# Opening turns, beta additions and the keys' pace reordered in a graph attention and top-p diffusion kernel

## Chip, cores and metric

The kernel runs on one core of one Trainium2 chip. The metric is device microseconds of one execution, and the time of a kernel is the median of its runs. A profile comes from one execution, and its span, the time between the program's first and last instruction, is somewhat shorter than that execution's own time.

## What is computed

There are 4096 nodes with 256 features each, and two layers. Both layers normalize the rows of x, apply a ReLU, and add their result to x. The first is a graph attention with four heads over the matrix adj; the second mixes plain graph diffusion (`Xf = R @ Xf`) and top-p attention over all nodes (`Xa = A @ Xa`), two steps of each.

```python
# layer 0, on h = relu(layernorm(x))
h = (h @ W).reshape(n, 4, 64)
src = einsum('nhd,d->nh', h, a[:64, 0]); dst = einsum('nhd,d->nh', h, a[64:, 0])
e = src[:, :, None] + dst.T[None, :, :]
e = where(adj > 0, where(e > 0, e, 0.2 * e), -9e15)
out = einsum('nhm,mhd->nhd', softmax(e, axis=-1), h)      # then
x = x + layernorm(out) * gamma + beta
# layer 1, on X = relu(layernorm(x)), Xf = Xa = X, Z = 0
R = row_normalized(adj + I)
for n in range(2):
    A = top_p_attention(Xa, W1, W2, W3)      # softmax(q k^T), the largest probabilities up to 0.9, renormalized
    Xf = R @ Xf
    Xa = A @ Xa
    Z = Z + Xf @ U1[n].T + Xa @ U2[n].T
x = x + layernorm(X + Z) * ln_g + ln_b
```

## The kernel before

The rows are held as 32 blocks of 128 (`NB`), in one tile `X` of 128 partitions. The order of every engine's instructions is the order in which the Python code issues them, since nearly all of it stands inside `tc.manual_schedule`; the framework adds the semaphore waits. What the code issues ahead of something else on the same engine is therefore executed ahead of it. SP's queue carries most loads and stores, POOL's queue the adjacency loads.

**The opening.** One turn (`turn_of(b)`) per block, and each turn works on several blocks at different stages: `opened(b + 2)` normalizes and rectifies a block on ACT (L233), `turned_rows(b + 1)` transposes it on PE (L240), `multiplied(b)` copies the transposed rows on ACT (L244) and multiplies them by `wx` on PE (L247). `wx` holds W and, in eight further columns, W times the two halves of `a`, which DVE works out first (L512, L514). `read(b - 1)` takes the eight logits out of PSUM (DVE, L251, into `sd_c`) and makes two exponentials per head of them (ACT, L254); `weighed(b - 1)` multiplies the block's rows by these (DVE, L259). `first_part`, `left`, `second_part` and `third_part` split the weighted rows in three bf16 parts (L263 and L270 on ACT, L267 on DVE, L275 on DVE and POOL), which POOL copies into `ut0` for head 0 (L276) and SP's queue stores for the other heads (L277). `measured(b + 8)` takes a block's moments (DVE, L149 and L150), and after each fourth block POOL makes the scales (`steps`, L141 to L144). Between turns 13 and 27, eight pieces of the first two sign tiles are made on POOL (`sign_stage` with a piece, L359).

**The attention passes.** For each group of 8 row blocks (`ig`) and each head there is one pass, 16 in all, each with 16 steps over pairs of neighbour blocks. A sign tile tells where `src + dst > 0` (ACT, L366, or DVE, L364); DVE ands it with the adjacency tile `ax` and takes the rest (L372, L373, two masks); PE multiplies both masks by the weighted rows into 8 PSUM banks (L392). Masks are made two steps ahead and signs three. `evacuate` empties the banks after a pass, and its later pieces wait in the list `later`, of which one is issued per step. After the last head of a group they include `closing(ig)`: moments of the rows (`stats`), then for each of 8 blocks `close(i)`, which normalizes (ACT, L441), multiplies by gamma (DVE, L442), adds beta to the old rows (POOL, L443), adds both (DVE, L444), stores `x1` (SP's queue) and takes moments, and then `relu` (ACT, L452). The last group's closing runs beside the first graph hop.

**The graph hops.** A hop has 4 passes over column groups of 8 blocks, with 32 steps each. `split` makes two parts of a block of rows, `hl` (L579 on ACT, L580 on DVE); `edge` loads a strip `ar` of the adjacency from DRAM (SP's queue, L572); `own` adds the identity (L589); PE multiplies (L602). At a pass's end `drained` copies four banks (L613) and, in the next pass, its rows are turned (L624).

**Beside the hop** the top-p attention is prepared by two generators, `fills` and `picks`; each half step of the hop advances `fills` by one `yield` and, except near the pass's end, `picks` too. `fills` begins with `projections`: for each of 8 groups of 4 blocks it transposes (L752 and L753), multiplies by the key and query weights (L759, L761), transposes keys and queries (L766, L768, L769) and takes their lengths. `yield from waits(k)` between these pieces sets their pace; n is the number of the diffusion step. Then follow the moments (L784), the tables, and logits and exponentials of the first three blocks, for which `picks` searches the threshold on DVE. After the hop, `attend` does the rest block by block.

Of the kernel before, what the change touches and what calls it, by code (L numbers as in the profile page):

```python
# [11 lines left out]
F32 = mybir.dt.float32  # L12
F32R = mybir.dt.float32r
# [13 lines left out]
P = 128  # L27
# [29 lines left out]
def gat_then_top_p_diffusion(  # L57
# [104 lines left out]
    with tc.tile_pool(name="l0", bufs=1) as l0, tc.tile_pool(name="l0s", bufs=2) as l0s, tc.tile_pool(name="l0o", bufs=1) as l0o:  # L162
# [26 lines left out]
        with tc.manual_schedule(engines=every | {ET.SP}):  # L189
# [31 lines left out]
            def measured(b):  # L221
                if b < NB:
                    if b % 4 == 0:
                        pro.mv = l0s.tile([P, 4, nc.vector.BN_AGGR_DIM], F32, name="mv4")
                    moments_of(pro.mv[:, b % 4, :], X[:, b, :])
                    if b % 4 == 3:
                        pro.scales[b // 4] = steps(pro.mv, 4, l0s)

            def opened(b):
                if b < NB:  # L230
                    rs, nmr = pro.scales[b // 4]
                    hb = pro.hb[b] = l0s.tile([P, D], F32, name="hb", tag="ob")
                    nc.scalar.activation(hb, X[:, b, :], AF.Relu, scale=rs[:, b % 4:b % 4 + 1], bias=nmr[:, b % 4:b % 4 + 1])  # L233
# [15 lines left out]
            def read(b):  # L249
                pm, uv = pro.pm[b], uvs[b % len(uvs)]  # L250
                nc.vector.tensor_scalar(sd_c[:, :, :, b], pm[:, ds(D, 2 * H)].rearrange("p (t h) -> p t h", t=2),  # L251
                                        TINY, -TINY, ALU.add, ALU.add)
                for t, scale in enumerate((1.0, ALPHA)):
                    nc.scalar.activation(uv[:, :, t, HD:], pm[:, ds(D + H, H)][:, :, None], AF.Exp, scale=scale)  # L254

# [47 lines left out]
            def turn_of(b):  # L303
# [34 lines left out]
        out_rows = {}  # L338
        later = []

        def sources(k):
# [11 lines left out]
        def signs(k, p, g=None, piece=None):  # L353

            g = g or l0m.tile([P, 2, G0 * P], U8, name="g", bufs=5)
            h = passes[k][1]
            if piece is not None:
                c, half = piece // 2, ts(piece % 2, G0 * P // 2)
                nc.gpsimd.tensor_scalar(g[:, c, half], shared[k].sr[:, half], d_neg[:, h, ds(2 * p + c, 1)], 255.0, ALU.is_gt, ALU.mult)  # L359
# [36 lines left out]
        def evacuate(k):  # L396
# [27 lines left out]
            return [three, divided] + (closing(ig) if h == H - 1 else [])  # L424

        def closing(ig):
            o = out_rows[ig]
# [9 lines left out]
            def close(i):  # L437
# [4 lines left out]
                nc.vector.tensor_mul(ob, ob, gamma_r)  # L442
                nc.gpsimd.tensor_tensor(xb, xb, beta_r, ALU.add)  # L443
                nc.vector.tensor_add(xb, xb, ob)  # L444
# [61 lines left out]
        with tc.manual_schedule(engines=every):  # L506
            for b in range(4):
                measured(b)
            for k in range(KC):
                for i in range(2):  # L510
                    pr = uvs[3 + i][:, :, 0, :HD]
                    nc.vector.tensor_mul(pr, wx[:, k, :D].rearrange("p (h d) -> p h d", h=H),  # L512
                                         a_r[:, None, ts(i, HD)].to_broadcast([P, H, HD]))
                    nc.vector.reduce_sum(wx[:, k, ds(D + i * H, H)], pr, axis=AX.X)  # L514
            for b in range(4, 8):
                measured(b)
# [10 lines left out]
            for n, (k, p) in enumerate(todo):  # L527
# [18 lines left out]
        ps1 = ctx.enter_context(tc.tile_pool(name="ps1b", bufs=2, space=PSUM))  # L546
        PASSES = NB // G0
        S = SimpleNamespace(spare=None)

        order = [(p, j) for p in range(PASSES) for j in range(NB)]  # L550

        def hop_of(hop):
            return SimpleNamespace(hop=hop, src={}, ar={}, hl={}, acc=None, begun=0, parted=0, owned=0)

        def source(A, n):
            if n in A.src or n >= len(order):
                return
            if A.hop == 0:
                A.src[n] = X[:, order[n][1], :]
            else:  # L560
                A.src[n] = S.rows.tile([P, D], F32, name="x1", bufs=3) if n % 5 < 3 else S.rows.tile([P, D], F32, name="xa")
                nc.sync.dma_start(A.src[n], xf_d[order[n][1]])

        def edge(A, n):
# [8 lines left out]
            A.ar[n] = ar  # L573

        def split(A, n):
            while A.parted < min(n, len(order)):
                src = A.src[A.parted]
                hl = rp.tile([P, 2, D], F32R, name="hl", bufs=5)
                nc.scalar.copy(hl[:, 0, :], src)  # L579
                nc.vector.tensor_tensor(hl[:, 1, :], src, hl[:, 0, :].bitcast(F32), ALU.subtract)  # L580
                A.hl[A.parted] = hl
                A.parted += 1

# [80 lines left out]

        first_hop = hops(hop_of(0))
        with tc.manual_schedule(engines=every | {ET.SP}):
# [50 lines left out]
    def waits(n):  # L717
        for i in range(n):
            yield

    def projections(cur, n, G):
# [25 lines left out]
        for g in range(NB // 4):  # L747
            xs = l1e.tile([P, 3, 4, P], F32, name="xs", tag="e1")
            for k in range(KC):
# [3 lines left out]
                nc.scalar.copy(xs[:, k], pt)  # L753
            yield from waits(1 + n)
            carried(xs, g, 0)
# [7 lines left out]
            carried(xs, g, 1)  # L763
            yield from waits(n)
            for i in range(4):
# [9 lines left out]
            carried(xs, g, 2)  # L775
            yield from waits(n)
            carried(xs, g, 3)
# [668 lines left out]
```

## Time and profile before

| What | us |
|---|---|
| Median of 3 runs (2898.01 to 2899.80) | 2899.59 |
| The profiled execution's own time | 2899.5 |
| Its span | 2897.7 |
| PE busy in it | 2814.0 (97%) |
| DVE busy | 2171.2 (75%) |
| ACT busy | 1914.8 (66%) |
| POOL busy | 878.6 (30%) |

The trace shows the stages in the order of time: the opening up to about 102 us, the attention passes to 810, the first hop with what stands beside it to 1124, the first top-p attention to about 1806, the second hop to about 2200, the second attention to the end. A busy share is an average over stages with different limits. In the profile's rows, a number in brackets with an arrow is how long the engine stood idle before an instruction, and what ended that; PEld is PE's weight load.

### The profile page before, as it was taken

The page shows a single profiled execution, that of the slowest core. Times are in us where ns is not written, and L with a number is a line of the kernel's source. Part 1 is how long each engine was busy: PE and PEld are TensorE (multiplying, and loading weights), DVE is VectorE, ACT ScalarE, POOL GpSimd, SP SyncE. Part 2 cuts the span into 40 slices and gives each one's busy share as a digit, 9 for nine tenths or more (in the row PEclk, how much of TensorE's full clock was granted, in tenths as well). Part 3 has the DMA queues.
Part 4 walks back from the last instruction along what each step waited for, and adds up shares of the span by engine and source line. Part 5 has one row for each costly group of instructions (what it writes and reads, how often), then busy time and mean ns, then how long its engine had stood idle before and what let it go on. Part 6 is the DMA issues. An engine that isn't in the chain of part 4 may idle for free. (4 is left out here: it accounts for less than half of the span.)

```text
span 2897.7 us, 51524 instructions
## 1 busy us (share of the span) xinstructions
PE 2814.0 (97%) x18777; PEld 2443.1 (84%) x18777; DVE 2171.2 (75%) x5069; ACT 1914.8 (66%) x3061; POOL 878.6 (30%) x1815
## 2 busy tenths in 40 slices
PE   6899999999999999999999999999999999999998
PEld 4799999999977778888888888767778888888887
DVE  7776877778654374888888889234474999999996
ACT  6786787868733634877788775222626777877782
POOL 6501211112010120233323331000204666666664
PEclk8899999999999999999999999999999999999999
DMA  7969577595454784000000000667992111111110
GB/s 177 217 247 223 187 227 195 211 224 187 177 189 158 238 298 164 20 20 26 20 20 20 26 20 19 231 197 236 313 352 68 31 31 38 34 31 31 39 31 25
DMA packets 190362, 376.48 MB, mean 130 GB/s; under 512 B 18192, under 2 KB 143120, under 8 KB 186000
## 3 DMA queue, kind: packets, MB, share of 16 engines
q1 hardware_dynamic: 146960, 275.12, 28.4%
q0 software_dynamic: 21504, 83.89, 12.2%
q10 hardware_dynamic: 21632, 14.05, 1.5%
q8 instruction: 152, 2.49, 0.3%
q14 instruction: 114, 0.93, 0.1%
HBM read 305.55 MB, written 113.57 MB: 145 GB/s over the span
## 5 line engine op out<-in xcount | busy, mean ns | idle before, releaser
L1075 PE MATMUL acc<-X,eT 128*128 128x256 f32 x4096 | 973.7, 383 | 3.3 <-ACT eT L1069 2.8
L1075 PEld LDWEIGHTS acc<-X,eT 128*128 128x128 f32 x4096 | 739.0, 190 | 111.4 <-ACT eT L1069 31.4
L392 PE MATMUL acc<-ut,m 128*128 128x195 bf16 (+1 forms) x8192 | 701.0, 247 | 8.2 <-DVE st L409 5.6
L392 PEld LDWEIGHTS <-m 128*128 128x128 fp8e4 x8192 | 696.4, 97 | 13.2 <-DVE st L409 4.7
L366 ACT ACTIVATE g<-sr,d_big 128x1024 uint8<-128x1024 f32 x444 | 467.7, 1139 | 2.6 <-DVE m L372 2.6
L890 ACT ACTIVATE e<-mm,nm 128x1024 f32<-128x1024 f32 x256 | 286.1, 1118 | 205.5 <-PE mm L707 204.1
L1069 ACT COPY eT<-tp 128x512 f32<-128x512 f32 x512 | 296.4, 580 | 89.7 <-PE tp L1067 89.6
L602 PE MATMUL mm<-ar,hl 128*128 128x512 f32 x844 | 341.8, 408 | 9.2 <-DMA ar<-adj_d 3.6
L976 DVE MAX8 cand<-big 128x8 f32<-128x228 f32 (+1 forms) x1152 | 348.3, 380 | 0.0
L958 DVE SCALAR_TENSOR_TENSOR big<-e,c 128x4096 f32<-128x4096 f32 x58 | 261.9, 4515 | 98.1 <-POOL c L943 58.8
L602 PE MATMUL acc<-ar,hl 128*128 128x512 f32 x844 | 328.3, 392 | 2.2 <-DVE ar L589 2.1
L914 POOL TENSOR_TENSOR sums<-sums 128x2 f32<-128x2 f32 x64 | 12.7, 198 | 1037.8 <-ACT void L897 1037.8
L1067 PE MATMUL tp<-ident,e 128*128 128x128 f32 x2048 | 306.1, 272 | 0.8 <-DVE e L1001 0.8
L1067 PEld LDWEIGHTS tp<-ident,e 128*128 128x128 f32 x2048 | 255.0, 140 | 60.4 <-PE acc L1085 1.2
L372 DVE TENSOR_TENSOR m<-g,ax 128x512 uint32<-128x512 uint32 x256 | 182.3, 712 | 115.5 <-PE acc L392 96.3
L897 ACT ACTIVATE void<-e,c1x 128x2048 int8<-128x2048 f32 x128 | 257.4, 2011 | 3.3 <-issue 2.5
L1001 DVE SCALAR_TENSOR_TENSOR e<-e,found 128x4096 f32<-128x4096 f32 x58 | 259.1, 4468 | 0.0
L897 ACT ACTIVATE void<-e,c 128x2048 int8<-128x2048 f32 x128 | 257.4, 2011 | 0.0
L707 PE MATMUL mm<-kT,qT 128*128 128x512 f32 x512 | 198.3, 468 | 3.6 <-ACT e L890 2.2
L602 PEld LDWEIGHTS mm<-ar,hl 128*128 128x128 f32 x844 | 158.8, 188 | 49.5 <-issue 9.2
L373 DVE TENSOR_TENSOR m<-m,ax 128x512 uint32<-128x512 uint32 x256 | 177.7, 694 | 26.0 <-DVE m L372 0.9
L602 PEld LDWEIGHTS acc<-ar,hl 128*128 128x128 f32 x844 | 158.8, 188 | 38.8 <-issue 4.1
(303 smaller groups left out, 3538.9 us busy)
## 6 DMA issues: line engine op xcount, KB each, us to landing
ar<-adj_d SPq DMA_DIRECT2D x211, 512.0 KB, 4.6
adj_d<-ax POOLq DMA_DIRECT2D x32, 2048.0 KB, 7.0
ut<-uv_d SPq DMA_DIRECT2D x60, 784.0 KB, 5.7
aru<-adj_d SPq DMA_DIRECT2D x45, 512.0 KB, 4.5
ax<-in_adj_t_dram POOLq DMA_DIRECT2D x32, 512.0 KB, 16.1
x<-xf_d SPq DMA_DIRECT2D x78, 128.0 KB, 4.9
xf<-xft_d SPq DMA_DIRECT2D x64, 128.0 KB, 2.2
sr<-s_d SPq DMA_DIRECT2D x15, 512.0 KB, 4.9
```

The lines of the kernel that those rows point to most:

```text
L366: nc.scalar.activation(g[:, c, :], shared[k].sr, AF.Relu, scale=BIG, bias=d_big[:, h, j:j + 1])
L392: nc.tensor.matmul(shared[k].acc[i][:, t, :cols], m[t][:, c, ts(i, P)], shared[k].ut[j // QUARTER][:, j % QUARTER, t, :cols], start=(j == ...
L602: nc.tensor.matmul(A.acc[c][s], A.hl[m][:, t, ts(s, P)], A.ar[m][:, ts(c, 512)], start=(j == 0 and t == 0), stop=(j == NB - 1 and t == 1))
L707: nc.tensor.matmul(pm[:, h, :], q[t], kT[:, ds(h * (N // 2) + c * 512, 512)], start=(t == 0), stop=(t == 1))
L890: nc.scalar.activation(ev[:, :, c, :], r.pm[c], AF.Exp, bias=r.nm, accum_out=r.sums[:, c // 2, c % 2:c % 2 + 1])
L897: nc.scalar.activation(void, r.e[:, ts(h, N // 2)], (AF.Relu, AF.Sign)[i], bias=r.c1, scale=-1.0, accum_out=r.sums[:, h, 2 + i:3 + i])
L958: nc.vector.scalar_tensor_tensor(big, r.e, r.c3, r.e, ALU.is_le, ALU.mult, accum_out=r.low3)
L976: nc.vector.max(cand[:, s, :], big[:, edges[s]:edges[s + 1]])
L1001: nc.vector.scalar_tensor_tensor(r.e, r.e, r.t, r.e, ALU.is_ge, ALU.mult, accum_out=kept)
L1067: nc.tensor.transpose(pt[:, i, :], r.e[:, ts(4 * g + i, P)], ident)
L1069: nc.scalar.copy(eT, pt)
L1075: nc.tensor.matmul(r.acc[:, 0, :], eT[:, i, :], cur[:, j, :], start=(j == 0), stop=(j == NB - 1))
```

## The change

- The first block of x is loaded alone, then blocks 1 to 3 in one load; `a` is loaded first on ACT's queue instead of second on SP's; w is loaded in two halves. The moments and scales of block 0 are made alone, then the first half of `wx`'s further columns, then blocks 1 to 3, then the second half.
- `read` issues the exponentials ahead of the logits' copy.
- The first two sign tiles are made on ACT in four halves (turns 14, 18, 22, 26) instead of on POOL in eight pieces, and `mask_stage(0)` is issued in turn 29 instead of 31.
- The beta additions leave `close` and are issued one per step on POOL in the passes of head 0 (12, 12 and 8 of them).
- The first five splits of the hop are issued with the first group's `relu` instead of at the hop's beginning in the code.
- `projections` yields more often in diffusion step 0 (twice instead of once, and once in two places with none before); in step 1 the numbers stay.

```diff
-            block_rows(0)
-            nc.scalar.dma_start(wx[:, :, :D], w.rearrange("(k p) m -> p k m", p=P))
-            nc.sync.dma_start(a_r, bass.AP(tensor=a.tensor, offset=a.offset, ap=[[0, P], [1, 2 * HD]]))
+            nc.sync.dma_start(X[:, 0, :], x[:P, :])
+            nc.scalar.dma_start(a_r, bass.AP(tensor=a.tensor, offset=a.offset, ap=[[0, P], [1, 2 * HD]]))
+            for k in range(KC):
+                nc.scalar.dma_start(wx[:, k, :D], w[ts(k, P), :])
+            nc.sync.dma_start(X[:, 1:4, :], x[P:4 * P, :].rearrange("(b p) d -> p b d", p=P))
...
-                    if b % 4 == 3:
+                    if b == 0:
+                        pro.first = [l0s.tile([P, 4], F32, name=f"{x}4") for x in ("rs", "nmr")]
+                        steps(pro.mv[:, :1], 1, l0s, *(t[:, :1] for t in pro.first))
+                    if b == 3:
+                        steps(pro.mv[:, 1:], 3, l0s, *(t[:, 1:] for t in pro.first))
+                    elif b % 4 == 3:
                         pro.scales[b // 4] = steps(pro.mv, 4, l0s)
...
             def read(b):
                 pm, uv = pro.pm[b], uvs[b % len(uvs)]
+                for t, scale in enumerate((1.0, ALPHA)):
+                    nc.scalar.activation(uv[:, :, t, HD:], pm[:, ds(D + H, H)][:, :, None], AF.Exp, scale=scale)
                 nc.vector.tensor_scalar(sd_c[:, :, :, b], pm[:, ds(D, 2 * H)].rearrange("p (t h) -> p t h", t=2),
                                         TINY, -TINY, ALU.add, ALU.add)
-                for t, scale in enumerate((1.0, ALPHA)):
-                    nc.scalar.activation(uv[:, :, t, HD:], pm[:, ds(D + H, H)][:, :, None], AF.Exp, scale=scale)
...
-                if 13 <= b < 29 and b % 2:
-                    n, piece = divmod((b - 13) // 2, 4)
-                    sign_stage(n, piece)
-                if b == NB - 1:
+                if 14 <= b < 30 and b % 4 == 2:
+                    sign_stage(*divmod(b // 4 - 3, 2))
+                if b == NB - 3:
                     mask_stage(0)
...
-            if piece is not None:
-                c, half = piece // 2, ts(piece % 2, G0 * P // 2)
-                nc.gpsimd.tensor_scalar(g[:, c, half], shared[k].sr[:, half], d_neg[:, h, ds(2 * p + c, 1)], 255.0, ALU.is_gt, ALU.mult)
-                return g
-            for c in range(2):
+            for c in range(2) if piece is None else (piece,):
...
-                nc.gpsimd.tensor_tensor(xb, xb, beta_r, ALU.add)
...
+                if ig == 0 and i0 < LOOK + 1:
+                    for b in range(i0, min(i0 + 2, LOOK + 1)):
+                        source(hop1, b)
+                        split(hop1, b + 1)
...
-            for b in range(4):
-                measured(b)
+            measured(0)
             for k in range(KC):
...
+                if k == 0:
+                    for b in range(1, 4):
+                        measured(b)
...
+                if k % H == 0 and 2 < p < PAIRS - 1 and lifted:
+                    b = lifted.pop(0)
+                    nc.gpsimd.tensor_tensor(X[:, b, :], X[:, b, :], beta_r, ALU.add)
...
-            yield from waits(1 + n)
+            yield from waits(2)
             carried(xs, g, 0)
...
             carried(xs, g, 1)
-            yield from waits(n)
+            yield
...
             carried(xs, g, 2)
-            yield from waits(n)
+            yield
             carried(xs, g, 3)
```

More of the change, by code (lines that the diff above doesn't have):

```diff
@@ L230, in opened @@
                 if b < NB:
-                    rs, nmr = pro.scales[b // 4]
+                    rs, nmr = pro.scales[b // 4] if b > 3 else pro.first
                     hb = pro.hb[b] = l0s.tile([P, D], F32, name="hb", tag="ob")
@@ L339, in gat_then_top_p_diffusion @@
         later = []
+        lifted = list(range(NB))
         def sources(k):
@@ L424, in evacuate, with hop_of, source, split @@
             return [three, divided] + (closing(ig) if h == H - 1 else [])
+        PASSES = NB // G0
+        S = SimpleNamespace(spare=None)
+        order = [(p, j) for p in range(PASSES) for j in range(NB)]
+        def hop_of(hop):
+            return SimpleNamespace(hop=hop, src={}, ar={}, hl={}, acc=None, begun=0, parted=0, owned=0)
+        def source(A, n):
+            if n in A.src or n >= len(order):
+                return
+            if A.hop == 0:
+                A.src[n] = X[:, order[n][1], :]
+            else:
+                A.src[n] = S.rows.tile([P, D], F32, name="x1", bufs=3) if n % 5 < 3 else S.rows.tile([P, D], F32, name="xa")
+                nc.sync.dma_start(A.src[n], xf_d[order[n][1]])
+        def split(A, n):
+            while A.parted < min(n, len(order)):
+                src = A.src[A.parted]
+                hl = rp.tile([P, 2, D], F32R, name="hl", bufs=5)
+                nc.scalar.copy(hl[:, 0, :], src)
+                nc.vector.tensor_tensor(hl[:, 1, :], src, hl[:, 0, :].bitcast(F32), ALU.subtract)
+                A.hl[A.parted] = hl
+                A.parted += 1
+        hop1 = hop_of(0)
         def closing(ig):
@@ L546, in gat_then_top_p_diffusion @@
         ps1 = ctx.enter_context(tc.tile_pool(name="ps1b", bufs=2, space=PSUM))
[L547 to L562, printed above, removed]
         def edge(A, n):
@@ L573, in edge @@
             A.ar[n] = ar
[L575 to L582, printed above, removed]
         def own(A, n):
@@ L663, in hops @@
             S.turned = turned
-        first_hop = hops(hop_of(0))
+        first_hop = hops(hop1)
         with tc.manual_schedule(engines=every | {ET.SP}):
```

## The prediction

> **What bounds the kernel now.** I read the page's row of busy slices first: PE has 9 in every slice but the first two and the last, so only stretches in which PE lacks work can give time back. Then I cut the start into stretches of 25 us (columns: stretch, length, then busy us and instructions of PE, PE's weight loads, DVE, ACT, POOL, then granted clock, DMA share, GB/s).
>
> ```profile
> 0.00:25.00 25.00, 11.44 (x44) 8.36 (x44) 16.36 (x55) 11.70 (x32) 9.39 (x54) 1.00 0.70 220
> 25.00:50.00 25.00, 16.65 (x62) 12.04 (x63) 20.74 (x63) 19.40 (x59) 19.40 (x30) 0.82 0.84 129
> 50.00:75.00 25.00, 18.70 (x53) 12.15 (x52) 20.81 (x60) 17.96 (x52) 23.91 (x32) 0.64 0.79 192
> 75.00:100.00 25.00, 18.51 (x50) 11.80 (x49) 18.36 (x45) 15.93 (x49) 24.35 (x31) 0.64 0.95 167
> 125.00:150.00 25.00, 25.00 (x297) 25.00 (x295) 15.99 (x36) 19.66 (x25) 1.29 (x2) 1.00 0.81 299
> ```
>
> From 125 us the attention passes keep PE full to 797 us, so nothing beside them counts there. Before it, in the opening (32 turns, one block of rows each), no engine is full except POOL from 50 to 100 us. There time goes round in waits. The timeline of one turn, then the waits up to 105 us (us in total, times, longest), then POOL's groups up to 130 us:
>
> ```profile
> 43.51 0.14 DVE L251 TENSOR_SCALAR sd_c<-b 128x8 f32<-128x8 f32 x1
> 43.75 0.24 ACT L254 ACTIVATE o<-b 128x4 f32<-128x4 f32 x2 [0.71 <-DVE sd_c L251]
> 44.09 0.76 DVE L259 TENSOR_TENSOR o<-b,o 128x256 f32<-128x256 f32 x2 [0.44 <-ACT o L254]
> ...
> ACT o L254 <- DVE sd_c L251: 14.7, 16, 2.4
> DVE o L259 <- ACT o L254: 5.3, 12, 0.8
> DVE o L259 <- POOL slots L275: 3.1, 3, 1.4
> ...
> L359 POOL TENSOR_SCALAR g<-sr,d_neg 128x512 uint8<-128x512 f32 x8 | 17.3, 2161 | 0.6
> ```
>
> The reader sees a ping-pong: ACT, ready 0.71 us earlier, waits for DVE's copy of the logits, and DVE then idles 0.44 us for ACT's exponentials. All rows of that waits view in which the weighting (L259) waits come to 5.3+1.6+1.2 = 8.1 us on ACT and 3.1+1.8+1.3+0.4+0.4 = 7.0 us on POOL, which is late with third parts (L275) behind its eight sign pieces. That is 15.1 us, the same as 75 us less DVE's 59.9 busy us from 25 to 100.
>
> Then the start, the end of the opening, and the stretch from 810 to 1124 us (first graph hop) in the timeline:
>
> ```profile
> 5.95 0.43 DVE L149 BATCH_NORM_STATS2 st<-X 128x6 f32<-128x256 f32 x1 [5.95 <-DMA X<-in_x_dram]
> 12.30 2.13 PE L247 MATMUL b<-wx,hT 128*128 128x264 f32 x4
> 102.17 0.10 PEld L392 LDWEIGHTS <-m 128*128 128x128 fp8e4 x1 [2.65 <-DVE m L372]
> ...
> 826.92 6.61 POOL L443 TENSOR_TENSOR X<-X,beta_r 128x256 f32<-128x256 f32 x8
> 828.74 0.77 DVE L444 TENSOR_TENSOR X<-X,ob 128x256 f32<-128x256 f32 x1
> 837.96 0.42 DVE L444 TENSOR_TENSOR X<-X,ob 128x256 f32<-128x256 f32 x1
> 839.94 0.47 PE L602 MATMUL mm<-ar,hl 128*128 128x512 f32 x1 [1.22 <-DMA ar<-adj_d]
> 901.46 0.47 PE L602 MATMUL mm<-ar,hl 128*128 128x512 f32 x1 [0.97 <-PE tp L752]
> 904.27 3.40 PE L759 MATMUL mm<-wkq,xs 128*128 128x128 f32 x16 [1.64 <-DVE stage L613]
> 912.11 1.12 PE L784 MATMUL mm<-e 128*64 128x65 f32 x16 [1.90 <-DVE qT L769]
> ```
>
> DVE begins at 5.95, the first projection stands at 12.30, the last (timeline) at 98.14 to 100.27, and attention waits until 102.17 for a mask. In the hop PE idles 16.1 us in all, counted from its rows between 795 and 1160 us.
>
> **What the Trainium skill says.** "PSUM — Partial Sum Buffer", section "PSUM bank collisions raise a hardware error": two engines may not touch one bank at once, and the scheduler makes an order "reads and writes alike: ACT↔DVE too". This explains why the exponentials wait for a copy whose result they do not read; the trace agrees (14.7 us above). "GPSIMD Engine Reference", section "Key points": POOL shares its SBUF interfaces with VectorE and contends with operations of two SBUF inputs; agreed: L444 takes 0.77 us beside POOL's beta additions and 0.42 us after them. "TensorE: Matmul & The Clock Gate", section "What's actually happening": an idle PE runs at half clock until some 3.4 us of work; agreed in kind, clock 0.64 from 50 to 100 us, where the four L247 matmuls take up to 2.13 us against 1.16 us.
>
> **The change, part by part.**
>
> *First block alone, constants' loads (start).* SP issues the same number of loads, the first 128 KB instead of 512 KB; a_r moves from SP to ACT's queue, and w is cut in two there, two issues more at about 0.5 us, which delay the loads of w1, w2 and wkq by 1 us; w1 is first used at 43 us, so nothing. No row shows a lone 128 KB load at the start; the page's xf loads of that size land in 2.2 us[...]. So block 0 lands near 3.3 us, the first half of w and a_r near 4 us (estimates; before, a_r landed at 7.3 us, behind the 512 KB). DVE's chain is the same 5.3 us (5.95 to 11.23) but cut: block 0, first half of w (1.6 us, to 5.7), blocks 1 to 3 (1.6 us, to 7.3), second half (1.6 us, to 8.9). POOL does its four scale steps twice, 2.2 us each (8.26 to 10.46 before): blocks 1 to 3 are scaled at 9.5 us. ACT's order puts the second opened block ahead of the first transposed copy, so the first projection follows at about 10.5 us. Gain 12.3 − 10.5 = **1.8 us**; bounds 0 (loads land as late as before) and 3.
>
> *Exponentials ahead of the copy.* DVE order stays, only the wait turns round: ACT's two exponentials wait for PE alone, DVE's copy waits for them. Queued behind that wait on DVE are the two weightings and a third part. ACT was ready 0.71 us early and the pair takes 0.24 us, so the copy finds it done. This takes the 8.1 us.
>
> *First signs on ACT.* Eight POOL operations (17.3 us) leave, four ACT activations of 1024 columns come, 1.14 us each (page, L366): 4.6 us in 16 turns. POOL falls from about 3 us a turn to 2, and its 7.0 us of lateness go. ACT's work in the turn shown ends 1.93 us after its exponentials' start (43.75 to 45.68 in the timeline); with 4.6/16 = 0.3 us of signs it stays below DVE's 2.75 − 0.44 = 2.31.
>
> *Mask stage 0 two turns earlier.* Its two DVE operations (1.21 and 0.88 us at 100.92) fall in a turn where DVE no longer measures (0.55 us less), and PE goes from the last projection straight into attention: 102.17 − 100.27 = **1.9 us**. POOL's small copy now waits for that mask, with three adjacency loads (0.75 to 0.87 us each) and third parts of blocks 26 and 27 behind it: about 2.6 us of POOL lateness, which DVE feels a turn later at most once; the adjacency itself (10 to 20 us to land) is needed over 25 us later. Cost 0 to 1, covered by POOL's spare.
>
> Of the 15.1 us I count four fifths, **12 us**: DVE at 2.31 us a turn will meet more POOL contention, and ACT's sign of 1.14 us in one turn of four can push the exponentials back. Bounds 4 and 15.1. Opening: 12 + 1.8 + 1.9 = **15.7 us**.
>
> *Beta additions moved* (32 POOL operations of 0.81 us, now in the first passes of head 0). There PE is full and DVE keeps two masks ahead; if that cover failed, 0.35 us of slower DVE each. In the last closing, three closes took 2.4 to 2.75 us against 1.86 us later: 3 × 0.75 = 2.3 us, and PE's three waits for ar (1.24, 0.82, 1.22), queued on SP behind the x1 stores of these closes, shrink. Gain **2.5 us**; bounds 0 and 3.3.
>
> *Splits moved.* Five ACT casts and DVE subtractions of 0.4 us already ran at 366 us beside full PE; they run there a little earlier, no time.
>
> *Keys' pace.* Six instead of three steps a group, 24 more steps for eight groups. The three waits at the pass end (0.97+1.64+1.90 = 4.5 us) fall apart, since group and pass end no longer meet as they did, and a dip of the clock behind them (3.40 against 2.1 us for L759), 1.3 us. But other ends now meet: group 3's transposed products at the first pass end, block 0's exponentials at the second, each holding a PSUM buffer for about 1.5 us; and DVE's last picks end after the last drain, 4.7 us late, before rows that PE takes 8 us to turn. Net gain **2 us**; bounds −3 and 6.
>
> Sum: 15.7 + 2.5 + 2 = 20.2 us. The profiled execution has 2897.7 us of span and 1.8 us around it, 2899.5, within 0.1 of the median of 2899.59. Predicted: 2899.5 − 20.2 = **2879 us**.
>
> **Rivals.** (1) The turn stops at 2.6 us: PE's own turn at half clock is 2.13 + 0.64 us, and DMA is already busy 0.79 to 0.95; for it, three of the last turns stood at 2.57; against it, faster turns raise PE's clock. Gain 31 × (2.77 − 2.6) = 5.3, +1.8+1.9+4.5: 2886 us. (2) The opening as forecast, but the keys' new pace only moves the waits (−1 instead of 2) and the closing keeps its waits: 2899.5 − 15.7 + 1 = 2885 us. (3) All hidden costs vanish: 18.8 + 3.3 + 6 = 28 us, 2871 us. (4) Slower: ACT becomes the bound of the opening. The weighting now stands behind PE, exponentials and copy in series; should ACT's turn grow by over 1.14 us (its lead of 0.71 and the old idle of 0.44), each turn is longer than before; at 0.8 us more a turn, 25 us, less 8 gained elsewhere: 2916 us. The added 0.3 us a turn speak against it. (5) The wait does not turn round and all but the closing's part is hidden: 2897 us.
>
> **How the numbers follow.** Forecast 0.55, rivals (1) and (2) 0.25, (3) 0.12, (5) 0.04, (4) 0.04. A measurement of this kernel tells about 0.2%, 5.8 us, from no change. Range 2869 to 2889 us: it takes in (1), (2) and (3). Faster by over 0.2% is all but (4) and (5): 0.92; within it 0.04, slower 0.04.
>
> **What would show it.** Right: turns of 2.3 to 2.5 us (L247's successor), no wait of ACT's exponentials for the logits' copy, POOL below 20 of 25 us, attention's first product near 86 us, no 0.77 us additions at the last closing. Wrong: turns of 2.6 us or more, waits of the copy for the exponentials over 0.4 us, masks or adjacency late in the first pass, PE idle over 14 us in the hop.

## Result and profile after

| | Before | After |
|---|---|---|
| Median of 4 runs, us | 2898.97 (2898.01 to 2899.80) | 2871.91 (2869.03 to 2874.37) |
| Ratio, 95% interval | | 0.9905 (0.989 to 0.992) |
| The profiled execution's own time, its span | 2899.5, 2897.7 | 2872.7, 2870.9 |

The kernel is 27 us faster; the forecast was 20 us, with a range that takes in the measured time. It got there with two terms far too small, one of the wrong sign and one put at nothing. One execution among those below, of the run named "The splits not moved", took 8787 us for no known reason, and its ratio leaves that one out. By stages, from the timelines of the two profiles:

| Stage (marks on PE) | Before | After | Gain | Forecast |
|---|---|---|---|---|
| Start to first projection | 12.30 | 14.16 | −1.9 | +1.8 |
| First to last projection, 31 turns | 85.84 | 73.49 | +12.35 | +12 |
| Last projection to attention's first product | 4.04 | 0.99 | +3.05 | +1.9 |
| Passes, to the hop's first product | 708.26 | 707.47 | +0.8 | 0 |
| First hop, to its last product | 312.64 | 300.77 | +11.9 | +4.5 |
| All behind it, to PE's last product | 1767.08 | 1767.15 | −0.1 | 0 |
| PE's last product to the end of the span | 7.56 | 6.88 | +0.7 | 0 |

The opening after the change, in the same stretches and columns as in the prediction (length, then busy us and instructions of PE, weight loads, DVE, ACT and POOL, then granted clock, DMA share, GB/s):

```profile
0.00:25.00 25.00, 10.99 (x44) 8.24 (x44) 15.63 (x53) 11.88 (x33) 10.06 (x58) 1.00 0.76 213
25.00:50.00 25.00, 15.64 (x66) 10.85 (x66) 24.20 (x69) 21.59 (x65) 21.17 (x32) 0.92 0.90 160
50.00:75.00 25.00, 17.98 (x66) 13.30 (x64) 24.41 (x71) 22.93 (x65) 21.51 (x36) 0.81 1.04 201
75.00:100.00 25.00, 21.02 (x155) 17.54 (x156) 23.81 (x50) 20.18 (x48) 18.86 (x27) 0.86 1.10 198
```

DVE, at 20.8 of 25 us before, is now at 24.2 to 24.4: the time in which it stood is gone, and DVE is the bound of the turns. The waits of DVE from 0 to 90 us say the same (us in total, times, longest). The 8.1 us for ACT's exponentials and the 7.0 us for POOL have become 2.7 us in which the copy waits for the exponentials:

```profile
DVE st L149 <- DMA X<-in_x_dram: 4.1, 1, 4.1
DVE sr L545 <- DMA wx<-in_w_dram: 3.0, 1, 3.0
DVE sd_c L260 <- ACT o L259: 2.7, 4, 0.9
```

The start, in the timeline after the change:

```profile
4.08 0.43 DVE L149 BATCH_NORM_STATS2 st<-X 128x6 f32<-128x256 f32 x1 [4.08 <-DMA X<-in_x_dram]
...
7.72 0.43 DVE L545 TENSOR_TENSOR sr<-wx,a_r 128x256 f32<-128x256 f32 x1 [2.99 <-DMA wx<-in_w_dram]
7.84 0.39 ACTq L206 DMA_DIRECT2D wkq<-in_w_t_dram  x1
8.28 0.60 ACT L240 ACTIVATE hb<-X,nmr,rs 128x256 f32<-128x256 f32 x1 [6.25 <-DMA X<-in_x_dram]
...
13.02 0.60 ACT L240 ACTIVATE hb<-X,nmr,rs 128x256 f32<-128x256 f32 x1 [4.14 <-POOL nmr L144]
...
14.15 1.97 PE L254 MATMUL b<-wx,hT 128*128 128x264 f32 x4
```

Block 0 is there at 4.08 us instead of 5.95, but the first half of w lands only at 7.7 us. (In the kernel before, all of w had landed at 5.7 and `a` at 7.3.) So DVE wins 1.9 us and then stands 3.0 us. The second opened block waits until POOL has made the scales of blocks 1 to 3, at 12.98 us, and the first transposed copy and the projection stand behind it in ACT's order. The scales of block 0 are ready at 6.27, yet ACT opens the block only at 8.28, directly behind its last issue of a load (`wkq`, at 7.84; at 2.40 in the kernel before). What held that issue the trace does not show; it did not set the first projection.

In the first hop the waits of PE (825 to 950 us) are these. The last closing's additions take 0.42 us, and the waits for `ar` behind them, three of 3.3 us in all before, are two of 1.3 us (0.9 us at 818, ahead of this stretch):

```profile
PE mm L615 <- DVE stage L626: 1.4, 1, 1.4
PE tp L765 <- ACT stage L645: 1.0, 1, 1.0
PE mm L797 <- DVE qT L782: 0.9, 1, 0.9
PE mm L615 <- DMA ar<-adj_d: 0.4, 1, 0.4
```

From the hop's first product to its last PE stands 7.6 us instead of 14.7 (the prediction's 16.1 took in waits outside the hop). That is 7.1 of the 11.9 us. The other 4.8 us are time in which the profile counts PE as busy with the same number of matmuls; 3.0 of them are in the products for keys and queries (L759, now L772), 15.6 us instead of 18.6. The passes look unchanged in sum and are not: the table's 0.8 us hides a gain of about 4 us and a loss of about as much, as the experiments show.

### The profile page after: what moved, and what is told of

It reads as the page before. It is cut to its first block, busy times and chain, and to the rows that moved or that the text cites. A ratio compares the mean times of both kernels' runs of the same rounds, so it can differ in the third digit from the quotient of the medians.

```text
span 2870.9 us, 51480 instructions
## 1 busy us (share of the span) xinstructions
PE 2798.5 (97%) x18777; PEld 2440.2 (85%) x18777; DVE 2169.1 (76%) x5069; ACT 1919.1 (67%) x3065; POOL 867.1 (30%) x1811
## 3 DMA queue, kind: packets, MB, share of 16 engines
q0 software_dynamic: 21504, 83.89, 12.3%
## 5 line engine op out<-in xcount | busy, mean ns | idle before, releaser
L395 PEld LDWEIGHTS <-m 128*128 128x128 fp8e4 x8192 | 696.1, 96 | 10.3 <-DVE m L376 6.1
```

Source lines behind the costliest of these rows:

```text
L395: nc.tensor.matmul(shared[k].acc[i][:, t, :cols], m[t][:, c, ts(i, P)], shared[k].ut[j // QUARTER][:, j % QUARTER, t, :cols], start=(j == ...
```

## Experiments

Each run is named against the changed or the earlier kernel. The medians of one kernel differ by up to 3 us between sets of runs (the changed kernel had 2871.91 and 2874.53), so totals closer than that are not told apart. The kernel before had 2898.97 in the first set and 2900.3 to 2900.8 in the later ones, so a distance from the changed kernel's first median is some 1.5 us too large. A stage is read from one profile of each, and that execution need not lie near the median of its set (the signs alone: 2898.14 us, median 2891.51). Two profiles of the changed kernel differ by 2.6 us behind the hop (1767.15 and 1769.77), and over all runs that leave that stretch as it is it took 1767.0 to 1772.3.

### The keys' pace, undone and alone

```diff
-            yield from waits(2)
+            yield from waits(1 + n)
...
-            yield
+            yield from waits(n)
```

> The changed kernel with the old pace of the keys (the waits of three or six steps a group as before). It should be 2872 us plus what the pace is worth. Theory A: the first hop's 11.9 us of gain are mostly the pace, since the gaps of PE at the two pass ends and at the drains come back: PE idle in the hop 9.1 to about 14 us, and the weight products for keys (L772) slow again, 13.6 to about 16.5 us; 2879 to 2881 us. Rival B, as forecast: the pace is worth 2 us, and the rest of the 11.9 us is the beta additions' or the clock's: 2874 us.

Measured: 2883.38 us, 0.9941 (0.9927 to 0.9954) of before, 11.5 us above the changed kernel's first median. The hop took 313.03 us instead of 300.77, PE stood 4.9 us more in it, and the products for keys took 19.0 us. The waits of PE from 825 to 950 us, then stretches of 5 us around them:

```profile
PE mm L797 <- DVE qT L782: 1.9, 1, 1.9
PE mm L772 <- DVE stage L626: 1.6, 1, 1.6
PE acc L615 <- DVE ar L602: 1.4, 1, 1.4
...
PE mm L615 <- PE tp L765: 1.0, 1, 1.0
```

```profile
880.00:885.00 5.00, 4.03 (x24) 3.12 (x22) 2.31 (x4) 2.86 (x6) 0.00 (x0) 1.00 0.69 200
885.00:890.00 5.00, 3.35 (x16) 3.12 (x15) 2.73 (x6) 1.26 (x4) 0.00 (x0) 0.63 0.04 13
890.00:895.00 5.00, 4.15 (x16) 3.13 (x14) 1.38 (x2) 0.99 (x2) 0.00 (x0) 0.69 0.30 84
895.00:900.00 5.00, 3.95 (x25) 3.02 (x26) 2.41 (x4) 0.77 (x3) 0.00 (x0) 0.66 0.05 21
```

The waits that the prediction showed are back, to the tenth. Two of them (1.0 and 1.65 us) lie within 3 us of each other at 883 to 887 us, and the granted clock (the figure behind POOL's) then stays at 0.63 to 0.69 for 15 us, in which a 128x512 product takes 0.63 us instead of 0.39. With the new pace PE waits 1.38, 1.01 and 0.93 us at 869, 893 and 912 us, far apart, and the clock stays at 1.00. Of the 12.3 us, 4.9 are waits; the other 7.3 are time in which PE counts as busy with the same matmuls. Theory A holds in its direction, and the total rose by more than it said.

The clock is only part of the 7.3 us. Five kept traces have the old pace and the same pair of waits: the kernel before, this run, and the exponentials, the signs and the beta additions alone, which follow below. Over the whole hop (length, then busy us of PE, weight loads, DVE, ACT and POOL, then the clock) stand here the kernel before, this run, the beta additions alone, the changed kernel and the new pace alone:

```profile
810.44:1123.08 312.64, 297.99 (x1478) 241.32 (x1479) 171.15 (x448) 127.79 (x269) 41.23 (x85) 0.99 0.70 235
794.94:1107.97 313.03, 300.51 (x1478) 243.55 (x1479) 168.56 (x448) 127.91 (x269) 34.59 (x77) 0.98 0.72 234
805.88:1114.22 308.34, 296.32 (x1478) 239.70 (x1479) 168.93 (x448) 128.07 (x269) 34.60 (x77) 1.00 0.74 238
796.11:1096.88 300.77, 293.19 (x1478) 240.58 (x1479) 164.08 (x442) 127.98 (x269) 32.95 (x77) 1.00 0.73 244
810.32:1113.45 303.13, 293.40 (x1478) 240.47 (x1479) 166.31 (x442) 127.99 (x269) 39.47 (x85) 1.00 0.76 242
```

In the third line the pair of waits stands at 894 to 898 us and the clock stays at 1.00 all the same. So about 4.2 of the 7.3 us (300.5 less 296.3) are the clock's in this one execution, and 3.1 us (296.3 less 293.2) belong to the old pace at full clock. For these the waits of the weight loads (PEld) offer a place. In the run of the third line, from 842 to 1000 us, they begin with the row below, where the key products stand behind ACT's copies of their rows; with the new pace no such row of the key products is left. That this makes up the 3.1 us is argued, not shown.

```profile
PEld mm L762 <- ACT xs L756: 4.0, 9, 0.6
```

> The kernel before with the keys' new pace alone. Theory A, from the run with the old pace: the gaps of PE at the pass ends (4.5 us) and the slow stretch of PE's clock behind them go wherever the hop stands, so 11 us less than before, and the weight products for keys (L759) take 13.6 us of PE instead of 16.6. Rival B: the pace was worth so much only beside the other moves, and alone it gives the 2 us of the forecast, with gaps of PE at other places in the hop.

Measured: 2890.93 us, 0.9969 (0.9957 to 0.9981), 9.3 us less than before. Hop 303.13 us (−9.5), products for keys 15.6 us, gaps again single ones of 1.38, 1.01 and 0.93 us. PE stands 9.7 us in the hop instead of 14.7, and counts as busy 4.6 us less. The pace needs none of the other moves.

### The beta additions, undone and alone

```diff
+                nc.gpsimd.tensor_tensor(xb, xb, beta_r, ALU.add)
                 nc.vector.tensor_add(xb, xb, ob)
...
-        lifted = list(range(NB))
+        lifted = []
```

> The changed kernel with the 32 beta additions back in the closes. Theory A: a pair of them on POOL stretches a mask of DVE to 2.15 us at three pass starts, so three gaps of PE of 1.3 us come back, one of 0.9 us at 117 us goes, and the closing behind the last pass waits 2 us longer: 3.9 - 0.7 - 0.9 + 2.0, about 4.3 us slower, 2876 us. As forecast, 2.5 us slower, 2874.5 us. Rival B: only the pass starts count, since the hop's gain is the pace's: 2874 us with PE's waits for ar behind the closing unchanged at 1.3 us.

Measured: 2882.21 us, 0.9938 (0.9924 to 0.9951), 10.3 us above the changed kernel's first median: more than each expectation. Passes 714.41 us (+6.9), hop 303.71 (+2.9). PE's gaps of over 0.3 us account for 4.2 of the 6.9 us in the passes. The three at pass starts are back (1.29, 1.28 and 1.27 us). The rest is not the additions' alone: the gap at 140 us, which the splits bring (below) and which differs from trace to trace, is 3.70 us here instead of 2.74, and the granted clock behind it, from 140 to 150 us, is 0.79 and 0.87 instead of 1.00. The remaining 2.7 us are time in which PE counts as busy; the run with the old start, whose clock is 0.66 from 140 to 145 us, has 2.6 us more of it than the changed kernel too.

> The kernel before with the beta additions moved and nothing else. Theory A: three gaps of PE of 1.3 us at pass starts go, and 2 to 3 us of the first hop's start: 6 to 7 us less than before. Rival B: all the 10 us that the undoing cost, 2890 us. As forecast: 2.5 us less, passes unchanged at 708 us.

Measured: 2891.95 us, 0.9971 (0.9961 to 0.9982), 8.8 us less than before: passes 704.18 us (−4.1), hop 308.34 (−4.3). Of the hop's 4.3 us, 2.6 are waits, mostly those for `ar` (1.1 us instead of 3.3), and 1.7 are PE's busy time, with the clock at 1.00 where it dipped before. What the forecast did not look for stands in the timeline of the kernel before, at the start of a pass:

```profile
320.34 2.15 DVE L372 TENSOR_TENSOR m<-g,ax 128x512 uint32<-128x512 uint32 x1
320.52 1.42 POOL L443 TENSOR_TENSOR X<-X,beta_r 128x256 f32<-128x256 f32 x2
...
323.75 1.44 PE L392 MATMUL acc<-ut,m 128*128 128x195 bf16 x13 [1.33 <-DVE st L409]
```

A pair of additions meets a mask, and the mask takes 2.15 us instead of 0.69. The difference, 1.46, is the pair's whole duration (1.42). The Trainium skill says this of POOL and DVE: in "SBUF — State Buffer", section "SBUF: two separate sides", the pair of ports that they share is an exclusive lock and not a split of bandwidth, and whichever operation starts first holds it for the whole instruction. The trace agrees in the length. It does not in the order: the mask's row starts 0.18 us ahead of the pair's, and the mask is still the one that grows. DVE is then late with emptying the banks of the pass before, and PE, full otherwise, stands 1.3 us, at 322, 500 and 676 us. The same rows are in the run with the additions put back (490.15, 2.14 us). With the additions moved, single ones fall at other times, and the gaps are gone at 500 and 676 us and 0.7 us instead of 1.3 at the first. One price is paid elsewhere: in the changed kernel, at 117 us in the first pass, two additions stretch two masks to 1.21 and 1.03 us, and PE stands 0.87 us. In this run, whose passes begin 13 us later, that gap is not there.

### The splits not moved

```diff
-                if ig == 0 and i0 < LOOK + 1:
-                    for b in range(i0, min(i0 + 2, LOOK + 1)):
-                        source(hop1, b)
-                        split(hop1, b + 1)
```

> The changed kernel without the splits moved into the closing of the first group of rows. Theory A: with the splits gone from there, the first addition of the identity to the adjacency is again behind them on DVE, so DVE does not wait for ar at 138 us and PE's gap of 2.7 us at 140 us goes, as do the three of 0.5, 1.1 and 0.5 us at 338 to 343 us; one of 1.6 us near 360 us comes back: 3.3 us faster, 2868.6 us. Rival B: the gap at 140 us is due to the faster opening and stays: 0.5 us faster. As forecast: no difference.

Measured: 2872.51 us, 0.9902 (0.9887 to 0.9917). The passes take 703.72 us, 3.75 less, as theory A has it: the gap at 140 us and the three at 338 to 343 us are gone, one of 1.73 us at 353 us is back. This profile gave the gain back later: 1.8 us in the hop and 5.1 us behind it, 2.3 of these in the second hop, with a clock of 0.91 from 2100 to 2120 us. The totals show no difference, and the stretch behind the hop differs by 2.6 us for the changed kernel itself. For the gap, the timeline of the changed kernel:

```profile
141.89 0.29 DVE L602 TENSOR_TENSOR ar<-ar,ident 128x128 fp32r<-128x128 f32 x1 [3.88 <-DMA ar<-adj_d]
...
142.84 3.32 PE L395 MATMUL acc<-ut,m 128*128 128x195 bf16 x37 [2.74 <-DVE m L376]
```

The hop's first addition of the identity (`own`) waits 3.88 us on DVE for a strip of the adjacency, and a mask stands behind it. Before, this addition ran at 367.8 us, behind the splits. The code's text did not move it; taking away what stood ahead of it did. This also limits what was said of the order at the start of the document: in the code the hop's first splits and additions stand behind all the passes, which end at 810 us, yet they ran in the middle of them. Across these two parts the place in the code does not tell when an operation runs.

### Exponentials alone, signs and mask alone

The first run makes only the edit of `read` in the kernel before, the second only those of `signs`, `turn_of` and `mask_stage`.

```diff
+                for t, scale in enumerate((1.0, ALPHA)):
+                    nc.scalar.activation(uv[:, :, t, HD:], pm[:, ds(D + H, H)][:, :, None], AF.Exp, scale=scale)
                 nc.vector.tensor_scalar(sd_c[:, :, :, b], ...
...
-                for t, scale in enumerate((1.0, ALPHA)):
-                    nc.scalar.activation(uv[:, :, t, HD:], pm[:, ds(D + H, H)][:, :, None], AF.Exp, scale=scale)
```

> The kernel before with one part of the change alone: the exponentials ahead of the logits' copy. Theory A, the sum of waits: the 8.1 us of waits for ACT go and the 7.0 us of POOL's lateness stay, so 31 turns take 85.8 - 8 = 78 us and the total is about 8 us less than that of before. Rival B: POOL, busy over 19 of 25 us, has become the next bound and takes the gain: 31 turns stay above 82 us, 4 us or less gained, and the weighting's waits for third parts grow beyond 7 us.

Measured: 2894.88 us, 0.9984 (0.9976 to 0.9992). 31 turns took 81.34 us, a gain of 4.5. Two stretches, then the waits of ACT from 20 to 96 us:

```profile
25.00:50.00 25.00, 15.94 (x67) 11.28 (x68) 24.39 (x71) 21.31 (x65) 22.67 (x34) 0.94 0.97 179
50.00:75.00 25.00, 16.45 (x52) 11.26 (x51) 19.21 (x58) 16.14 (x48) 23.99 (x32) 0.72 0.83 154
```

```profile
ACT o L252 <- POOL slots L275: 8.3, 5, 2.5
ACT o L252 <- POOL st L275: 2.5, 2, 1.3
ACT uv L252 <- POOL st L275: 2.4, 2, 1.4
ACT sr L252 <- POOL st L275: 1.5, 1, 1.5
ACT uv L252 <- POOL slots L275: 1.3, 1, 1.3
```

Up to 50 us the turns run as fast as DVE can. Then POOL's eight sign pieces begin, POOL is at 24 of 25 us, and the exponentials wait 16.0 us for third parts. Both theories were half right: the ping-pong is gone, and POOL takes part of the gain.

```diff
-                if 13 <= b < 29 and b % 2:
...
-                if b == NB - 1:
+                if 14 <= b < 30 and b % 4 == 2:
+                    sign_stage(*divmod(b // 4 - 3, 2))
+                if b == NB - 3:
                     mask_stage(0)
...
```

> The kernel before with one other part alone: the first signs on ACT and mask stage 0 two turns earlier. Theory A: the 7.0 us of POOL's lateness go and the ping-pong of 8.1 us stays, so 31 turns take about 79 us; with the earlier mask (3 us from the last projection to the first product) the total is 9 to 10 us less than that of before. Rival B: ACT's signs of 1.14 us come into a turn in which ACT and DVE wait for each other, and the turns gain under 4 us.

Measured: 2891.51 us, 0.9968 (0.9956 to 0.998). 31 turns took 82.92 us, a gain of 2.9; attention's first product follows 1.92 us after the last projection begins instead of 4.04, so 2.1 more. POOL fell to 19 to 21 of 25 us, and the ping-pong stayed (ACT's exponentials on the copy, 20 to 96 us):

```profile
ACT o L254 <- DVE sd_c L251: 8.3, 13, 1.2
ACT uv L254 <- DVE sd_c L251: 3.6, 4, 2.2
ACT sr L254 <- DVE sd_c L251: 2.0, 5, 0.9
```

Rival B's bound held. Alone the two give 4.5 and 2.9 us, together 12.35: each takes away what hides the other.

### What bounds the turns now

```diff
-                    moments_of(pro.mv[:, b % 4, :], X[:, b, :])
+                    if b < 8:
+                        moments_of(pro.mv[:, b % 4, :], X[:, b, :])
```

> The changed kernel without the row moments (BATCH_NORM) of blocks 8 to 31; their rows are scaled with the numbers of blocks 4 to 7, and POOL computes these as often as before. DVE loses 24 times 0.53 us, 12.7 us, in the opening. Theory A: DVE, busy 24.4 of 25 us, is the bound of the turns now; they fall until ACT (22.9 of 25) or POOL holds them, from 2.39 to 2.1 to 2.2 us, 31 turns to 66 to 69 us and the total by 5 to 8 us. Rival B: DVE is busy because it is stretched beside the others, and PE at its low clock or the loads set the turn: 31 turns stay at 73 to 74 us.

Measured in the opening: 31 turns in 68.15 us (2.20 each), attention's first product at 82.72 instead of 88.64. DVE falls to 22.6 of 25 us, and ACT rises to 24:

```profile
25.00:50.00 25.00, 16.96 (x75) 12.02 (x74) 22.66 (x57) 23.94 (x73) 23.51 (x37) 0.94 1.00 183
50.00:75.00 25.00, 16.32 (x67) 11.76 (x66) 22.59 (x54) 24.21 (x69) 23.66 (x39) 0.91 1.10 212
```

Theory A holds: DVE was the bound. Taking 12.7 us of work from it gave 5.3 us, and then ACT and POOL are the fullest, at 24 and 23.5 of 25 us: the next bound stands 7% behind DVE. The total, 3110.39 us, tells nothing of this: with other scales the data are others, and behind 2,860 us, where the changed kernel is done, a search on DVE is still running (31 scans of 4.5 us).

### The start

The first run takes back the whole edit of the start:

```diff
-            nc.sync.dma_start(X[:, 0, :], x[:P, :])
...
+            block_rows(0)
...
-            measured(0)
+            for b in range(4):
+                measured(b)
```

> The changed kernel with the old start: four blocks in the first load, w in one load, a_r on SP, four blocks measured first. Theory A: the new start lost 1.9 us, so the first projection moves from 14.2 to 12.3 us and the total falls to about 2870 us. Rival B: the later first projection is made good by later turns, which DVE sets, so the first attention product stays at 88.6 us within 0.5 and the total at 2872 us. As forecast it would be 1.8 us slower, 2874 us.

Measured: 2872.09 us, 0.9899 (0.9884 to 0.9914). First projection at 12.28, first attention product at 86.44, 2.2 us before that in the changed kernel's first profile and 1.5 before that in its second (87.98, below); the total does not resolve it.

The second makes another start:

```diff
-            nc.sync.dma_start(X[:, 0, :], x[:P, :])
+            nc.sync.dma_start(X[:, :2, :], x[:2 * P, :].rearrange("(b p) d -> p b d", p=P))
...
-            for k in range(KC):
-                nc.scalar.dma_start(wx[:, k, :D], w[ts(k, P), :])
+            nc.scalar.dma_start(wx[:, :, :D], w.rearrange("(k p) m -> p k m", p=P))
...
-            nc.scalar.dma_start(w1_s, ...
+            nc.sync.dma_start(w1_s, ...
```

> The changed kernel with two things mended: the splits not moved, and a start in which two blocks are loaded first, w comes in one load behind a_r on ACT's queue, the loads of w1, w2 and wkq move to SP, and blocks 2 and 3 are measured after w's products. Theory: ACT's first opening no longer stands behind issues of loads, the second opened block has its scales with the first, so the first projection is at 10.5 to 11.5 us instead of 14.2; with 3.7 us from the splits, 6 us less than the changed kernel, 2866 us. Rival: the turns take the earlier start back and the second hop's clock takes the splits' part, as in the run without them: 2871 to 2872 us.

Measured: 2871.53 us, 0.9897 (0.9882 to 0.9912). The first projection stands at 11.70 (a little later than expected), 2.5 us before the changed kernel's, and attention's first product at 88.09, only 0.55 before. The first projection was the wrong mark. Stretches of 10 us of the old start (e2), of this one (e7) and of the changed kernel, in this order:

```profile
0.00:10.00 10.00, 0.00 (x0) 0.00 (x0) 3.86 (x13) 1.28 (x1) 3.43 (x42) 1.00 0.70 215
10.00:20.00 10.00, 8.18 (x32) 5.93 (x33) 9.19 (x32) 7.80 (x25) 3.51 (x9) 1.00 0.99 301
```

```profile
0.00:10.00 10.00, 0.00 (x0) 0.00 (x0) 2.48 (x8) 1.39 (x2) 3.23 (x43) 1.00 0.70 214
10.00:20.00 10.00, 7.97 (x25) 5.61 (x26) 8.97 (x33) 5.86 (x18) 3.12 (x8) 1.00 1.06 281
```

```profile
0.00:10.00 10.00, 0.69 (x2) 0.29 (x2) 2.79 (x9) 1.88 (x2) 3.05 (x43) 1.00 0.75 225
10.00:20.00 10.00, 6.33 (x22) 5.08 (x23) 8.12 (x30) 5.00 (x17) 3.40 (x8) 1.00 1.02 275
```

DVE has done 13.05, 11.45 and 10.91 us of work by 20 us. The leads over the changed kernel, 2.14 and 0.54 us, are those of attention's first product, 2.20 and 0.55. The other kept traces with these turns say the same: DVE's busy us up to 20 us and the time of attention's first product add up to 99.5 (99.48 to 99.66) in all seven in which attention begins within 1.2 us of the last projection's first matmul, whichever start they have. With DVE as the bound, the start is worth what DVE gets done in it. The changed kernel's own start varies, though: five profiles with it had 10.91 to 12.02 us of DVE's work by 20 us, and e7's 11.45 lies between them. Only the old start, with 13.05 and 12.99 in its two profiles, stands apart.

### A faster version

The old start and the splits at their old place, as above, and:

```diff
-                if k % H == 0 and 2 < p < PAIRS - 1 and lifted:
+                if k % H == 1 and 2 < p < PAIRS - 1 and lifted:
```

> The changed kernel with the old start, the splits not moved, and the lifted beta additions in the passes of head 1 instead of head 0. Theory: what each gave in a single profile adds up: first attention product at 86.5 us instead of 88.6, the passes 3.7 us shorter by the splits, 0.9 us by the beta additions that no longer lie beside the masks of the first pass (gap of PE at 117 us); the hop begins at 789 us instead of 796 and the total is 6 us below the changed kernel's, 2866 us. Rival: it comes back in the rest, as with e4 and e7; the hop begins at 789 us, but the total is 2870 us or more.

Measured: 2866.50 us, 0.9882 (0.9867 to 0.9897). The hop begins at 788.18 us, no gap of PE is left at 117 or 140 us, and the rest takes 1767.14 us.

> The changed kernel itself, for a comparison on one chip: 2872 us, 0.9905 of before. If its stretch after the first hop again takes 1767 us, the 1770 to 1772 us of e2, e4 and e7 are theirs; if it takes 1770, they are not.

Measured: 2874.53 us, 0.9913 (0.9899 to 0.9926), and 1769.77 us behind the hop. So the 1767 to 1772 us of that stretch are not told apart by the edits. Beside it on the same chip the version with the old start, the splits at their old place and the additions in the passes of head 1 is 8 us faster; it beats both kernels. In the two profiles 6.8 us are gained by the hop's beginning (788.18 instead of 794.95), by the three edits together; another 2.6 us behind the hop are not theirs to claim.

## Why the prediction was right, and where it was not

- **Exponentials and signs, 12 us: right, 12.35.** The turns take 2.37 us, the copy of the logits ends no wait of the exponentials, POOL is at 21.2 to 21.5 of 25 us where under 20 was forecast. One sign of being wrong came and meant little: the copy waits up to 0.9 us for the exponentials, in four turns. Counting both waits as one sum of 15.1 us was right only because both parts were in the change: alone they gave 4.5 and 2.9, not 8.1 and 7.0. DVE's load set the end, as the forecast's 2.31 us a turn had it. Rival 1 (turns stop at 2.6) and rival 4 (ACT the bound) are out, though ACT is 7% from it.
- **First block alone, +1.8: wrong, −1.9.** The failed step is the landing of w's first half and `a_r` "near 4 us": they landed at 7.7 and 5.6. The estimate took a load by itself, while other loads were in flight; which of them held w was not tried. This one step accounts for the miss: the loads came 3.7 us late, the scales of blocks 1 to 3 are at 12.98 us instead of 9.5, and the projection, behind the second opened block in ACT's order, at 14.15 instead of 10.5 (13.45 to 13.95 in four more profiles with this start). And the first projection was the wrong mark in any case: what counts is DVE's work by 20 us. Attention's first product came at 88.64, not near 86.
- **Mask stage 0 earlier, 1.9: 3.05.** The wait of 1.9 us is gone; the 1.1 us more are mostly the clock at the last projection, whose four matmuls take 1.16 us instead of 2.13.
- **Beta additions, 2.5: 8.4.** In the closing the forecast was right: by the run alone the hop gave 4.3, of which the waits for `ar` are 2.2 and PE's busy time, with no dip of the clock, 1.7. The 4.1 us of the passes were put at nothing. The failed sentence is "there PE is full": full on average, with three gaps of 1.3 us that a list of PE's gaps would have shown, and POOL's additions beside each. In the first pass the forecast's doubt came true: with masks late there, PE stands 0.87 us at 117.
- **Splits, no time: −3.75 in the passes.** The step looked only at the cast and the subtraction. These had kept the hop's `own` out of the masks' way on DVE, which was not in the step; and at their new place DVE waits for ACT's casts (1.51 us at 336 and at 340) while PE stands at 338 to 343 us.
- **Keys' pace, 2: 9.5, by the run with the pace alone.** Waits: 4.9 us, near the forecast's 4.5, but not where it had them. The three of 4.5 us at the first pass end have become three single ones of 3.3 us, so part of the feared new meetings did come; a wait of 1.4 us at 950 us is gone, and those at the second pass end fall from 3.2 to 1.25 us, which the forecast did not name. Clock: put at 1.3 us, it is about 1.7 us in the kernel before (PE busy 297.99 us in the hop, 296.32 where the clock did not dip). Missing: the 2.9 us that PE counted as busy at full clock. So the failed step is the 3.8 us of counter-costs that were taken off, and the time behind ACT's copies that was put at nothing. Rival 2, which had the pace cost a microsecond, is out.

With these terms the sum is 12.35 − 1.9 + 3.05 + 8.4 − 3.75 + 9.5 = 27.7 us, against 26.8 in the spans; the clock's 1.7 us in the hop are counted in both 8.4 and 9.5. That the total fell in the range is partly luck: two terms missed by 3.7 us each on one side, two by 4 to 6 and by 7.5 us on the other. Rival 3 named this total (2871 us), with the hidden costs gone from closing and pace, but not the reasons.

## What to carry to other kernels

When two waits alternate in one loop, price them together and name the engine that is full when both are gone; here a single fix showed less than half. Then judge the stage ahead of these turns by what that engine gets done in it, not by the first result. Ahead of a move, list the bottleneck's gaps over the whole run, also where it is busy by 97%, with the engine that runs beside each; an operation that seems free may be what holds another one back. And before a dip of the clock in one profile is put down to the code, look whether other profiles with the same waits have it.

## What was not expected of the hardware

- The same two gaps of PE, of 1.0 and 1.65 us within 3 us, stand in five traces. They were followed by 15 us at a granted clock of 0.63 to 0.69 (old pace in the changed kernel), by 15 us at 0.60 to 0.74 (signs alone), by 5 us at 0.69 (kernel before) and at 0.66 (exponentials alone), and by none in the fifth (beta additions alone, 1.00). Single gaps of 1.38 us left it at 1.00 in the changed kernel and with the new pace alone. What decides between none, 5 and 15 us is open; no run repeats a profile of one kernel with the old pace.
- At the start, 512 KB of x landed at 5.9 us and 128 KB alone at 4.1, but the first 256 KB alone only at 7.0 (e7). Which of the loads in flight held that one was not tried.
- In several places a mask on DVE grew by about the whole length of POOL's additions beside it, not by a share: from 0.69 to 1.45 us beside one of 0.74 (at 310 us in the changed kernel), to 2.15 beside two, and to 4.58 beside six in a row (4.14 us, at 145 us in the faster version, with no gap of PE there). Where masks and additions took turns each grew by less (masks to 1.03 to 1.23 us, additions from 0.72 to 1.17, at 108 to 118 us in the changed kernel).
